# Summing the last four batches of a recurrent block with v on TensorE, in pieces woven among the projections

## The chip, the cores and the metric

The kernel runs on one core of a Trainium2 chip. The metric is device time in microseconds (us) of one execution; several runs are given by their median. The profile comes from one further execution of its own.

## The reference

Eight batches of 256 tokens with 512 channels go through a transformer block (self-attention, cross-attention, MLP) and then an RWKV block, of which the second half of the time is spent. The part that the change touches is its time mixing. For each of 32 heads with 16 channels:

```
def step(s, rkvw):
    r_t, k_t, v_t, w_t = rkvw
    a = k_t[..., :, None] * v_t[..., None, :]
    out = jnp.einsum('bhi,bhij->bhj', r_t, u * a + s)
    s = a + w_t[..., :, None] * s
    return (s, out)
...
_, out = jax.lax.scan(step, s0, rkvw)
out = jnp.moveaxis(out, 0, 1).reshape(b, l, e)
og = out.reshape(b, l, h, s_)
m = og.mean(-1, keepdims=True)
va = ((og - m) ** 2).mean(-1, keepdims=True)
og = ((og - m) / jnp.sqrt(va + 1e-05)).reshape(b, l, e) * gn_w + gn_b
x1 = x + og * g @ Wo.T
...
kk = jnp.square(jax.nn.relu(xk2 @ Wfk.T))
return x1 + rr * (kk @ Wfv.T)
```

r, k, v, w and g are projections of five mixtures of the layer-normalised input; the channel mixing at the end has three more projections (Wfr, Wfk, Wfv).

## The kernel before

Tokens of a batch lie in chunks of 16. Time mixing takes a batch through these stages, all written for the "time" set of buffer slots:

- `a`: layer norm, the shifted difference and the small tanh products that make the mixtures.
- `b` and `e`: the projections g and k, then v, w and r (`proj_t`, `proj_n`, three matmuls a product by `mm3`, L185 to L187). Each result goes to DRAM in a layout by head groups.
- `c`: reads k, r, w back with (head group, chunk) on partitions and makes, inside every chunk, the matrix A of scores between its 16 positions. POOL multiplies into a scratch tile X (L713, L714, L724, L737), DVE reduces X into A (L715, L730, L743), POOL scales r and k by decays (L747 to L749). Then the sum of A with v: 16 POOL products of growing width (L755, 64 up to 1,024 elements a partition) and a DVE reduction behind each (L762). Results go back to DRAM: `ks`, `r0`, `dd` and the in-chunk output `on` (L766, L770).
- `d`: the part between chunks. Small 32x32 TensorE products make each chunk's update of the state (L807), a DVE scan runs over the chunks (L824), small products apply r to the states (L834), DVE adds them to the in-chunk output that was read back (L837), and a group normalisation without the scale follows, written to `yg`.
- `f` and `g`: channel mixing, "chan" slots. `f` reads `yg`, gates it, projects with Wo (L185 to L187 into `o`), adds the residual (L902), layer-normalises (two POOL instructions, L197 and L198) and splits; `g` has the three large projections and the store of the output. In the first `f` the four weights of 512x512 are loaded and split in two parts (L171, L172).

Everything is written in Python in the order of `SEQ`; each entry is a stage letter and a batch. Two numbers decide the real order: the stage's priority, which is batch plus `AT[stage]` times 1,000 (the lower, the more urgent), and the scheduler that puts every instruction into its engine's queue when its inputs are there by the scheduler's own estimate of time. On the chip each queue is then run in that order. `c` and `d` have the most urgent values (-9.5 and -9.3), `f` and `g` late ones (6.25 and 7.75). All DMAs are issued from SP's queue. Buffers are named slots: `in:a16-a19` are the four tiles that a `c` reads, `staged` tiles come from a pool of two.

Of the kernel before, what the change touches and what calls it, by code (L numbers as in the profile page):

```python
# [10 lines left out]
ALU = mybir.AluOpType  # L11
# [6 lines left out]
P = 128  # L18
# [21 lines left out]
def slots(text):  # L40

    r = {}
    for item in text.split():
# [18 lines left out]
        "in:a16-a19 ob:a12 vm:a20,a21 r0t:a22 sts:a23 on_:a2 "  # L62
# [9 lines left out]
    "a0 b0 a1 e0 c0 b1 a2 e1 c1 d0 b2 a3 e2 c2 d1 b3 a4 e3 c3 d2 b4 a5 e4 c4 d3 b5 a6 e5 c5 d4 b6 a7 e6 c6 d5 b7 "  # L72
    "e7 c7 f0 d6 f1 g0 d7 f2 g1 f3 g2 f4 g3 f5 g4 f6 g5 f7 g6 g7"
# [12 lines left out]
PACE = 1000  # L86

# [5 lines left out]
def block_kernel(ctx: ExitStack, tc: tile.TileContext, a: dict, out: bass.AP):  # L93
# [162 lines left out]
    def proj_t(w, xt, emit, kind="o", noc=4, pairs=False):  # L256

        (wh, wl), (xh, xl) = w, xt
        for o2 in range(noc // 2):
            o = bank(kind, [P, 2, T])  # L260
            for oo in range(2):
                oc = 2 * o2 + oo
                cs = slice(oc * P, (oc + 1) * P)
                for k in range(KC):
                    mm3(o[:, oo, :], wh[:, k, cs], wl[:, k, cs], xh[:, k, :], xl[:, k, :], k == 0, k == KC - 1)
                if not pairs:
                    emit(oc, o[:, oo, :])
            if pairs:
                emit(slice(2 * o2, 2 * o2 + 2), o)

    def proj_n(ws, xts, emit, kind="o"):

        for t in range(2):
            ts = slice(t * P, (t + 1) * P)
            o = bank(kind, [P, D])
            n = len(ws)
            for u in range(n):
                (wh, wl), (xh, xl) = ws[u], xts[u]
                for k in range(KC):
                    mm3(o, xh[:, k, ts], xl[:, k, ts], wh[:, k, :], wl[:, k, :], u == 0 and k == 0, u == n - 1 and k == KC - 1)  # L280
            emit(t, o)
# [257 lines left out]
    class TimeMix:  # L539
# [119 lines left out]
        def e(self, b, got):  # L659
# [28 lines left out]
        def c(self, b, got):  # L688
# [3 lines left out]
            def from_dram(src):  # L692
                d_ = wt("in", [P, 16, 64])
# [3 lines left out]
            kb, rb, wb = (from_dram(z) for z in (kd, rd, wd))  # L697

            vt = wt("in", [P, 64, 16])
            for h in range(2):  # L700
                vh = staged([P, 8, 64])
                nc.sync.dma_start(out=vh, in_=vd.rearrange("e (c t) d -> (e c) t d", t=16)[:, 8 * h : 8 * h + 8, :])
                S.copy(vt[:, :, 8 * h : 8 * h + 8].rearrange("p d s -> p s d"), vh)


            A = wt("A", [P, 16, 16, 4])

            def part(t, s_, dims):
                return bass.AP(A.tensor, A.offset + 64 * t + 4 * s_, [A.ap[0], *dims])
# [5 lines left out]
            V.tensor_reduce(part(0, 0, [[68, 16], [1, 4]]), X.rearrange("p (t g i) -> p t g i", t=16, i=16), AX.X, ALU.add)  # L715


            for m in (1, 2, 4, 8):
                nb = 8 // m
                R, K, Wd = (z.rearrange("p (n u) d -> p n u d", n=nb) for z in (rb, kb, wb))  # L720
                if m < 4:
                    for i in range(m):
# [7 lines left out]
                        V.tensor_reduce(part(m + i, 0, [[136 * m, nb], [1, 4 * m]]), X.rearrange("p (n g i) -> p n g i", n=nb, i=16), AX.X, ALU.add)  # L730
                else:
                    ni = 16 // m
                    for n in range(nb):
                        for i in range(0, m, ni):
# [8 lines left out]
                            V.tensor_reduce(part(t0, s0, [[64, ni], [1, 4 * m]]), X.rearrange("p (n g i) -> p n g i", n=ni, i=16), AX.X, ALU.add)  # L743
# [7 lines left out]
            ob = wt("ob", [P, 16, 64])  # L751
            for t in range(16):
                n = t + 1
                Y = wt("X", [P, 1024])[:, : 64 * n] if t else ob[:, 0, :]
                G.tensor_tensor(  # L755
                    Y.rearrange("p (h j s) -> p h j s", h=4, j=16),
                    A[:, t, 0:n, :].rearrange("p s h -> p h s").unsqueeze(2).broadcast_to([P, 4, 16, n]),
                    vt[:, :, 0:n].rearrange("p (h j) s -> p h j s", j=16),
                    ALU.mult,
                )  # L760
                if t:
                    V.tensor_reduce(ob[:, t, :], Y.rearrange("p (d s) -> p d s", s=n), AX.X, ALU.add)  # L762
# [8 lines left out]
            return back(kb, "ks"), back(rb, "r0"), dd, vd, back(ob, "on")  # L771

        def d(self, b, got):

            ksd, r0d, dd, vd, ond = got
# [50 lines left out]
            for q in range(4):  # L826
# [9 lines left out]
                for par in range(2):  # L836
                    V.scalar_tensor_tensor(ov, op.rearrange("p t g c j -> p (t g) c j")[:, :, par], pm[:, 2 + par : 3 + par], ov, ALU.mult, ALU.add)  # L837

# [117 lines left out]
    def mix(n):  # L956
        for _ in range(min(n, len(seq))):
# [3 lines left out]
            with tc.high_priority(tc.cur_priority - base[0] - int(PACE * (b + AT[stage]))):  # L961
                if stage in "fg":
# [12 lines left out]
    mix(len(seq))  # L975

# [51 lines left out]
```

## Time and profile before

| what | us |
|---|---|
| median of 3 runs | 1974.78 |
| lowest and highest | 1973.81, 1986.49 |
| the profiled execution's own time | 1982.31 |
| its span, first to last instruction | 1980.5 |
| stage `c` on POOL, first instruction of batch 0 and last of batch 7 | 1239.2 and 1794.4 |
| the same for batches 4 to 7 | 1520.5, 1588.9, 1662.1, 1727.9 (starts) |
| last large product of `e` for batch 7 | 1638.9 |
| `yg` of batch 7 written | 1833.4 |
| last four periods of channel mixing | about 33 each |

"Busy" is the time in which an engine has an instruction; a matmul's end is modelled, so neighbouring matmuls overlap in the rows and the distance between two starts is what one costs. The granted clock is the share of full speed that TensorE had. A window row has, after its length, each engine's busy time and instructions, then granted clock, DMA share and GB/s.

### The profile page before, as it was taken

The numbers are of one execution on the slowest core, as the hardware profiler recorded it, in microseconds if no ns is written. First come the engines' busy times: TensorE is split into PE (matmuls) and PEld (weight loads), VectorE is DVE, ScalarE is ACT, GpSimd is POOL, SyncE is SP. The second block draws the span as 40 slices with busy tenths as digits, with TensorE's granted clock in tenths as the row PEclk, the third lists the DMA queues.
The fourth block names the chain that finished last, engine by engine and source line by source line (L and its number), as shares of the span: only waits on it lengthen the run. The fifth ranks groups of instructions, "written<-read, shape, count | busy, mean of one in ns | idle before, by whom it ended". The sixth has DMA issues, their size and how long they took to land.

```text
span 1980.5 us, 38765 instructions
## 1 busy us (share of the span) xinstructions
PE 1756.4 (89%) x14576; PEld 1471.8 (74%) x14576; DVE 1379.7 (70%) x3211; ACT 1106.5 (56%) x2745; POOL 747.5 (38%) x550
## 2 busy tenths in 40 slices
PE   4999999989999998999999988888889895789877
PEld 4777777777777776799999976676777673677766
DVE  4777777776778687665654454669678788888554
ACT  3877777887778688532332334354464454355342
POOL 2111111121221221232311100898899999992000
PEclk9999999999999999999999998988898886888888
DMA  6644444656555556322311133454556476442210
GB/s 189 158 125 119 118 118 125 190 142 164 132 146 143 133 135 207 110 90 69 107 65 64 54 128 103 116 142 125 157 138 165 130 195 184 142 108 97 75 64 22
DMA packets 237170, 247.35 MB, mean 125 GB/s; under 512 B 156292, under 2 KB 159244, under 8 KB 236983
## 3 DMA queue, kind: packets, MB, share of 16 engines
q1 hardware_dynamic: 236982, 244.87, 44.7%
q8 instruction: 115, 1.88, 0.4%
q14 instruction: 73, 0.59, 0.1%
HBM read 118.71 MB, written 58.98 MB: 90 GB/s over the span
## 4 chain that ended last, share of the span: by engine, by line
PE 60%; DVE 15%; DMA 6%; ACT 6%; POOL 5%; issue 3%; SPq 3%; POOLq 0%; DVEq 0%; ACTq 0%
PE o L185 8%; PE o L186 8%; PE o L187 8%; PE mm L185 5%; PE mm L186 4%; PE mm L187 4%; PE tr L366 3%; PE out L187 3%; PE out L186 3%; PE out L185 3%; DVE e L359 3%; POOL X L755 2%; PE cx L375 2%; DVE e L357 2%; PE sc L355 2%
## 5 line engine op out<-in xcount | busy, mean ns | idle before, releaser
L362 ACT ACTIVATE e<-e,mx 128x256 f32<-128x256 f32 x512 | 256.7, 506 | 43.0 <-DVE mx L359 42.0
L357 DVE TENSOR_TENSOR e<-sc,mc 128x512 f32<-128x512 f32 x256 | 172.1, 683 | 111.8 <-PE sc L355 56.2
L227 POOL TENSOR_TENSOR u<-y,u 128x1024 fp32r<-128x1024 f32 x32 | 78.5, 2452 | 440.8 <-ACT u L226 440.6
L359 DVE CUSTOM_DVE_ANT_0 e<-e,mn 128x256 f32<-128x256 f32 x512 | 220.6, 473 | 1.0
L755 POOL TENSOR_TENSOR X<-A,in 128x128 f32<-128x128 f32 (+14 forms) x120 | 209.3, 1779 | 14.7 <-DVE ob L762 12.4
L185 PE MATMUL o<-whi,s 128*128 128x512 f32 x320 | 148.4, 464 | 49.4 <-ACT s L890 31.8
L366 PE MATMUL tr<-ident,e 128*128 128x128 f32 x1024 | 174.7, 285 | 18.0 <-ACT e L362 14.7
L185 PE MATMUL mm<-u,whi 128*128 128x256 f32 x512 | 153.7, 301 | 14.3 <-DVE s L319 7.8
L370 ACT COPY pt<-tr 128x512 f32<-128x512 f32 x256 | 147.0, 582 | 34.6 <-PE tr L366 33.9
L366 PEld LDWEIGHTS tr<-ident,e 128*128 128x128 f32 x1024 | 122.3, 144 | 49.2 <-ACT e L362 24.2
L186 PE MATMUL mm<-u,whi 128*128 128x256 f32 x512 | 147.5, 288 | 4.0 <-POOL u L227 4.0
L185 PE MATMUL o<-u,whi 128*128 128x256 f32 x512 | 144.7, 287 | 3.1 <-ACT whi L171 1.6
L187 PE MATMUL mm<-u,wlo 128*128 128x256 f32 x512 | 147.0, 287 | 0.0
L186 PE MATMUL o<-u,whi 128*128 128x256 f32 x512 | 144.0, 283 | 0.0
L187 PE MATMUL o<-u,wlo 128*128 128x256 f32 x512 | 144.0, 283 | 0.0
L186 PE MATMUL o<-wlo,s 128*128 128x512 f32 x320 | 141.4, 442 | 0.0
L293 POOL TENSOR_TENSOR xr<-xr,row 128x512 f32<-128x512 f32 x48 | 65.7, 1388 | 186.0 <-DMA xr<-in_x 81.1
L355 PE MATMUL sc<-stk 128*128 128x256 f32 x512 | 118.0, 322 | 19.3 <-DVE e L357 13.9
L187 PE MATMUL o<-whi,s 128*128 128x512 f32 x320 | 134.4, 438 | 0.6 <-DVE s L891 0.5
L507 ACT ACTIVATE hf<-o,cv 128x256 f32<-128x256 f32 x128 | 59.8, 475 | 117.8 <-PE o L187 115.0
L197 POOL TENSOR_SCALAR rstd<-mv 128x2 f32<-128x2 f32 x48 | 17.2, 357 | 281.2 <-DVE mv L195 260.5
L185 PEld LDWEIGHTS o<-whi,s 128*128 128x128 f32 x320 | 70.0, 219 | 68.8 <-ACT s L890 33.3
(324 smaller groups left out, 5296.3 us busy)
## 6 DMA issues: line engine op xcount, KB each, us to landing
stk<-s SPq DMA_DIRECT2D x512, 128.0 KB, 2.4
x<-x SPq DMA_DIRECT2D x40, 512.0 KB, 4.7
x<-xr SPq DMA_DIRECT2D x24, 512.0 KB, 3.6
xr<-x SPq DMA_DIRECT2D x16, 512.0 KB, 4.8
w<-in_w SPq DMA_DIRECT2D x16, 512.0 KB, 6.7
w<-v SPq DMA_DIRECT2D x32, 256.0 KB, 3.2
x<-in_x SPq DMA_DIRECT2D x8, 512.0 KB
xr<-in_x SPq DMA_DIRECT2D x8, 512.0 KB, 3.6
```

The lines of the kernel that those rows point to most:

```text
L185: TE.matmul(o, ah, bh, start=first, stop=False)
L186: TE.matmul(o, ah, bl, start=False, stop=False)
L187: TE.matmul(o, al, bh, start=False, stop=last)
L227: (eng or V).tensor_tensor(lo, y, r32(hi), ALU.subtract)
L293: G.tensor_tensor(x[:, t, :], x[:, t, :], r, ALU.add)
L355: TE.matmul(sc[:, t, :], qs[hm][:, hc, t * P : (t + 1) * P], ks[hm][:, hc, :], start=True, stop=True)
L357: V.tensor_tensor(e, sc, mc, ALU.mult)
L359: V.tensor_tensor_reduce(e[:, t, :], e[:, t, :], mn[:, t, :], 1.0, 3.0e38, ALU.add, ALU.min, accum_out=mx[:, kk2, hc, t : t + 1])
L362: S.activation(pr[:, t, :], e[:, t, :], AF.Exp, bias=mx[:, kk2, hc, t : t + 1], scale=-1.0, accum_out=sums[:, kk2, hc, t : t + 1])
L366: TE.transpose(pt_ps[:, kk, t * P : (t + 1) * P], pr[:, t, kk * P : (kk + 1) * P], ident)
L370: S.copy(pt, pt_ps)
L755: G.tensor_tensor(Y.rearrange("p (h j s) -> p h j s", h=4, j=16), A[:, t, 0:n, :].rearrange("p s h -> p h s").unsqueeze(2).broadcast_to([P ...
```

## The change

Batches 0 to 3 stay as they were. For batches 4 to 7 (`LATE = 4`):

- `c` no longer loads v, and its 16 products with v (L755) and 16 reductions (L762) are gone. A is laid out the other way round (source position outermost, then head, then target position); one A tile is shared by the four batches, and set to zero once on POOL. It is written to DRAM (`own`) in place of `on`.
- `d` becomes a generator, `steps`. It reads A back with (chunk, source position) on partitions, spreads it with ScalarE into two masked halves (`Ax`, two instructions a half of the tokens), and TensorE multiplies it with v: 32 heads, four 32-row products each, for both halves of the tokens, 256 products of 32x32 by 32x16 a batch (`inside`). ScalarE copies the sum into `o`, where it was read from DRAM before. The rest of `d` (updates, scan, `across`, normalisation) is kept.
- `steps` stops at each `yield` with a number of columns. `between`, called behind each triple of large matmuls, counts the columns that those streamed and lets the next piece be written when the number is reached. A woven piece so takes the priority of the stage in which it is written. `finish(b)` writes out what is left before `f` of that batch.
- `SEQ` has `d4` behind `a7`, `d5` behind `c7`; the slots of the tiles that `c` reads get names of their own on the same addresses.

```diff
-        "in:a16-a19 ob:a12 vm:a20,a21 r0t:a22 sts:a23 on_:a2 "
+        "kb:a16 rb:a17 wb:a18 vt:a19 ob:a12 At:a19 Ax:a12 vm:a20,a21 r0t:a22 sts:a23 on_:a2 "
...
-    "a0 b0 a1 e0 c0 b1 a2 e1 c1 d0 b2 a3 e2 c2 d1 b3 a4 e3 c3 d2 b4 a5 e4 c4 d3 b5 a6 e5 c5 d4 b6 a7 e6 c6 d5 b7 "
-    "e7 c7 f0 d6 f1 g0 d7 f2 g1 f3 g2 f4 g3 f5 g4 f6 g5 f7 g6 g7"
+    "a0 b0 a1 e0 c0 b1 a2 e1 c1 d0 b2 a3 e2 c2 d1 b3 a4 e3 c3 d2 b4 a5 e4 c4 d3 b5 a6 e5 c5 b6 a7 d4 e6 c6 b7 e7 c7 "
+    "d5 f0 f1 g0 d6 f2 g1 d7 f3 g2 f4 g3 f5 g4 f6 g5 f7 g6 g7"
...
+LATE = 4
...
+    woven, columns = [], [0]
+    def between(n):
+        columns[0] += n
+        while woven and columns[0] >= woven[0][1]:
+            columns[0] -= woven[0][1]
+            was, phase[0] = phase[0], "time"
+            woven[0][1] = next(woven[0][2], None)
+            if woven[0][1] is None:
+                woven.pop(0)
+            phase[0] = was
+    def weave(b, steps):
+        if not woven:
+            columns[0] = 0
+        woven.append([b, 0, steps])
+    def finish(b):
+        while woven and woven[0][0] <= b:
+            columns[0] = woven[0][1]
+            between(0)
...
                     mm3(o[:, oo, :], wh[:, k, cs], wl[:, k, cs], xh[:, k, :], xl[:, k, :], k == 0, k == KC - 1)
+                    between(3 * T)
...
                     mm3(o, xh[:, k, ts], xl[:, k, ts], wh[:, k, :], wl[:, k, :], u == 0 and k == 0, u == n - 1 and k == KC - 1)
+                    between(3 * D)
...
                 TE.matmul(tp_[0:64, 0, :], d1[:, k, :], y[:, k, :], start=k == 0, stop=k == KC - 1)
+                between(4 * T)
...
+            late = b >= LATE
+            if not late:
...
+            if b <= LATE:
+                self.A = wt("A", [P, 1024])
+            if b == LATE:
+                G.memset(self.A, 0.0)
+            A = self.A
+            st_, ss, sh = (1, 64, 16) if late else (64, 4, 1)
...
-            ob = wt("ob", [P, 16, 64])
-            for t in range(16):
-                n = t + 1
-                Y = wt("X", [P, 1024])[:, : 64 * n] if t else ob[:, 0, :]
-                G.tensor_tensor(
-                    Y.rearrange("p (h j s) -> p h j s", h=4, j=16),
-                    A[:, t, 0:n, :].rearrange("p s h -> p h s").unsqueeze(2).broadcast_to([P, 4, 16, n]),
-                    vt[:, :, 0:n].rearrange("p (h j) s -> p h j s", j=16),
-                    ALU.mult,
-                )
-                if t:
-                    V.tensor_reduce(ob[:, t, :], Y.rearrange("p (d s) -> p d s", s=n), AX.X, ALU.add)
+            if not late:
+                At = A.rearrange("p (t s h) -> p t s h", t=16, s=16)
+                ob = wt("ob", [P, 16, 64])
...
+            if late:
+                own = dtile(f"ad_{b}", [P, 16, 64])
+                nc.sync.dma_start(out=own, in_=A.rearrange("p (s x) -> p s x", s=16))
+            return back(kb, "ks"), back(rb, "r0"), dd, vd, own if late else back(ob, "on")
...
+            if b >= LATE:
+                return weave(b, self.steps(b, got))
...
+        def steps(self, b, got):
+            ksd, r0d, dd, vd, ad = got
+            dn = staged([16, D])
+            nc.sync.dma_start(out=dn.rearrange("c (e d) -> c e d", e=8), in_=dd.rearrange("e c d -> c e d"))
+            s0t = wt("s0t", [P, KC, 16])
+            nc.sync.dma_start(out=s0t, in_=a["ctx"][b, 2:18, :].rearrange("r (a j) -> (r a) j", j=16).rearrange("(g p) j -> p g j", p=P))
+            ks = [self.n_tile(ksd, t, "ks") for t in range(2)]
+            At = wt("At", [P, 2, 8, 64])
+            for t in range(2):
+                nc.sync.dma_start(out=At[:, t], in_=ad.rearrange("(e u c) s x -> u (c s) e x", e=8, u=2)[t])
+            r0 = [self.n_tile(r0d, t) for t in range(2)]
+            o = wt("on_", [P, 2, D])
+            yield 8 * T
+            dt_ps = bank("wtp", [P, KC, 16])
+            for k in range(KC):
+                TE.transpose(dt_ps[:, k, :], dn[:, k * P : (k + 1) * P], ident[:16, :16])
+            dts = wt("dts", [P, KC, 16])
+            G.memset(dts[:, :, 0:1], 0.0)
+            S.copy(dts[:, :, 1:16], dt_ps[:, :, 0:15])
+            centred(s0t.rearrange("p g j -> p (g j)"), KC, bank("wtp", [P, KC]))
+            sts = wt("sts", [P, KC, 32, 16])
+            for hp in range(2):
+                S.activation(sts[:, :, 16 * hp : 16 * hp + 16, 0], s0t, AF.Copy, scale=pm[:, hp : hp + 1])
+            r0t = wt("r0t", [P, KC, T])
+            yield 4 * T
+            for k2 in range(2):
+                tp = bank("wtp", [P, 2, T])
+                for kk in range(2):
+                    for t in range(2):
+                        TE.transpose(tp[:, kk, t * P : (t + 1) * P], r0[t][:, (2 * k2 + kk) * P : (2 * k2 + kk + 1) * P], ident)
+                S.copy(r0t[:, 2 * k2 : 2 * k2 + 2, :], tp)
+                if not k2:
+                    yield 8 * T
+            vms, vns = [], []
+            for t in range(2):
+                vms.append(wt("vm", [P, 2, D]))
+                vns.append(self.n_tile(vd, t))
+                for par in range(2):
+                    S.activation(vms[t][:, par, :], vns[t], AF.Copy, scale=pm[:, 2 + par : 3 + par])
+            def spread(t):
+                Ax = wt("Ax", [P, 32, 2, 16])
+                for par in range(2):
+                    S.activation(Ax[:, :, par, :], At[:, t].rearrange("p e (h t) -> p (e h) t", t=16), AF.Copy, scale=pm[:, 2 + par : 3 + par])
+                return Ax
+            yield 28 * T
+            for r_ in range(4):
+                rws = slice(32 * r_, 32 * r_ + 32)
+                up = bank("up", [P, 2, KC, 2, 32])
+                for t in range(2):
+                    for g in range(KC):
+                        for q in range(4):
+                            ch = slice(g * P + 32 * q, g * P + 32 * q + 32)
+                            TE.matmul(up[32 * q : 32 * q + 32, t, g], ks[t][rws, ch], vms[t][rws, :, ch], start=True, stop=True)
+                for t in range(2):
+                    c0 = 1 + 8 * t + 2 * r_
+                    n = min(2, 16 - c0)
+                    for hp in range(2):
+                        js = slice(16 * hp, 16 * hp + 16)
+                        S.activation(sts[:, :, js, c0 : c0 + n].rearrange("p g j c -> p g c j"), up[:, t, :, 0:n, js], AF.Copy, scale=pm[:, hp : hp + 1])
+                if r_ == 3:
+                    Ax = spread(0)
+                yield 9 * T
+            for g in range(KC):
+                dT = bank("up", [P, 32, 16])
+                S.copy(dT, dts[:, g, :].unsqueeze(1).broadcast_to([P, 32, 16]))
+                sv = sts[:, g].rearrange("p j c -> p (j c)")
+                V.tensor_tensor_scan(sv, dT.rearrange("p j c -> p (j c)"), sv, 0.0, ALU.mult, ALU.add)
+            def inside(t):
+                av = bank("wtp", [P, D])
+                for h in range(32):
+                    js = slice(16 * h, 16 * h + 16)
+                    for pr in range(4):
+                        rws = slice(32 * pr, 32 * pr + 32)
+                        TE.matmul(av[rws, js], Ax[rws, h].rearrange("p c t -> p (c t)"), vns[t][rws, js], start=True, stop=True)
+                    if h % 4 == 3:
+                        if h == 31:
+                            S.copy(o[:, t, :], av)
+                        yield 5 * T
+            def across(q):
+                rws = slice(32 * q, 32 * q + 32)
+                op = bank("up", [P, 2, KC, 2, 32])
+                for t in range(2):
+                    for g in range(KC):
+                        for pr in range(4):
+                            c0 = 8 * t + 2 * pr
+                            at = t * P + 32 * pr
+                            TE.matmul(op[32 * pr : 32 * pr + 32, t, g], r0t[rws, g, at : at + 32], sts[rws, g, :, c0 : c0 + 2].rearrange("p j c -> p c j"), start=True, stop=True)
+                    if t and q:
+                        chosen(q, op)
+                    elif t:
+                        first.append(op)
+                    yield 6 * T
+            def chosen(q, op):
+                ov = o.rearrange("p t (g q j) -> p (t g) q j", q=4, j=32)[:, :, q]
+                for par in range(2):
+                    V.scalar_tensor_tensor(ov, op.rearrange("p t g c j -> p (t g) c j")[:, :, par], pm[:, 2 + par : 3 + par], ov, ALU.mult, ALU.add)
+            first = []
+            yield from inside(0)
+            Ax = spread(1)
+            yield from across(0)
+            yield from inside(1)
+            chosen(0, first[0])
+            for q in range(1, 4):
+                yield from across(q)
+            self.normed(b, o)
...
+                if stage == "f":
+                    finish(b)
...
+    finish(len(jobs))
```

More of the change, by code (lines that the diff above doesn't have):

```diff
@@ L690, in c, with from_dram @@
             rd, kd, vd, wd = got
-            def from_dram(src):
-                d_ = wt("in", [P, 16, 64])
+            def from_dram(src, name):
+                d_ = wt(name, [P, 16, 64])
                 nc.sync.dma_start(out=d_, in_=src.rearrange("e (c t) d -> (e c) t d", t=16))
                 return d_
[L697 to L706, printed above, removed]
+            kb, rb, wb = (from_dram(z, n) for z, n in ((kd, "kb"), (rd, "rb"), (wd, "wb")))
+            late = b >= LATE
+            if not late:
+                vt = wt("vt", [P, 64, 16])
+                for h in range(2):
+                    vh = staged([P, 8, 64])
+                    nc.sync.dma_start(out=vh, in_=vd.rearrange("e (c t) d -> (e c) t d", t=16)[:, 8 * h : 8 * h + 8, :])
+                    S.copy(vt[:, :, 8 * h : 8 * h + 8].rearrange("p d s -> p s d"), vh)
+            if b <= LATE:
[4 more added lines that the diff above has]
+            st_, ss, sh = (1, 64, 16) if late else (64, 4, 1)
             def part(t, s_, dims):
-                return bass.AP(A.tensor, A.offset + 64 * t + 4 * s_, [A.ap[0], *dims])
+                return bass.AP(A.tensor, A.offset + st_ * t + ss * s_, [A.ap[0], *dims])
             X = wt("X", [P, 1024])
@@ L714, in c @@
             G.tensor_tensor(X3, X3, W["ubc"].unsqueeze(1).broadcast_to([P, 16, 64]), ALU.mult)
-            V.tensor_reduce(part(0, 0, [[68, 16], [1, 4]]), X.rearrange("p (t g i) -> p t g i", t=16, i=16), AX.X, ALU.add)
+            V.tensor_reduce(part(0, 0, [[st_ + ss, 16], [sh, 4]]), X.rearrange("p (t g i) -> p t g i", t=16, i=16), AX.X, ALU.add)
             for m in (1, 2, 4, 8):
@@ L729, in c @@
                         )
-                        V.tensor_reduce(part(m + i, 0, [[136 * m, nb], [1, 4 * m]]), X.rearrange("p (n g i) -> p n g i", n=nb, i=16), AX.X, ALU.add)
+                        V.tensor_reduce(part(m + i, 0, [[2 * m * (st_ + ss), nb], [ss, m], [sh, 4]]), X.rearrange("p (n g i) -> p n g i", n=nb, i=16), AX.X, ALU.add)
                 else:
@@ L742, in c @@
                             )
-                            V.tensor_reduce(part(t0, s0, [[64, ni], [1, 4 * m]]), X.rearrange("p (n g i) -> p n g i", n=ni, i=16), AX.X, ALU.add)
+                            V.tensor_reduce(part(t0, s0, [[st_, ni], [ss, m], [sh, 4]]), X.rearrange("p (n g i) -> p n g i", n=ni, i=16), AX.X, ALU.add)
                 wl_ = Wd[:, :, m - 1 : m, :]
@@ L749, in c @@
                 G.tensor_tensor(wr_, wr_, wl_, ALU.mult)
-            ob = wt("ob", [P, 16, 64])
-            for t in range(16):
-                n = t + 1
-                Y = wt("X", [P, 1024])[:, : 64 * n] if t else ob[:, 0, :]
-                G.tensor_tensor(
-                    Y.rearrange("p (h j s) -> p h j s", h=4, j=16),
-                    A[:, t, 0:n, :].rearrange("p s h -> p h s").unsqueeze(2).broadcast_to([P, 4, 16, n]),
-                    vt[:, :, 0:n].rearrange("p (h j) s -> p h j s", j=16),
-                    ALU.mult,
-                )
-                if t:
-                    V.tensor_reduce(ob[:, t, :], Y.rearrange("p (d s) -> p d s", s=n), AX.X, ALU.add)
+            if not late:
+                At = A.rearrange("p (t s h) -> p t s h", t=16, s=16)
+                ob = wt("ob", [P, 16, 64])
+                for t in range(16):
+                    n = t + 1
+                    Y = wt("X", [P, 1024])[:, : 64 * n] if t else ob[:, 0, :]
+                    G.tensor_tensor(
+                        Y.rearrange("p (h j s) -> p h j s", h=4, j=16),
+                        At[:, t, 0:n, :].rearrange("p s h -> p h s").unsqueeze(2).broadcast_to([P, 4, 16, n]),
+                        vt[:, :, 0:n].rearrange("p (h j) s -> p h j s", j=16),
+                        ALU.mult,
+                    )
+                    if t:
+                        V.tensor_reduce(ob[:, t, :], Y.rearrange("p (d s) -> p d s", s=n), AX.X, ALU.add)
             def back(src, name):
@@ L770, in c @@
             nc.sync.dma_start(out=dd.rearrange("e c d -> (e c) d"), in_=wb[:, 15, :])
-            return back(kb, "ks"), back(rb, "r0"), dd, vd, back(ob, "on")
+            if late:
+                own = dtile(f"ad_{b}", [P, 16, 64])
+                nc.sync.dma_start(out=own, in_=A.rearrange("p (s x) -> p s x", s=16))
+            return back(kb, "ks"), back(rb, "r0"), dd, vd, own if late else back(ob, "on")
         def d(self, b, got):
+            if b >= LATE:
+                return weave(b, self.steps(b, got))
             ksd, r0d, dd, vd, ond = got
@@ L837, in d @@
                     V.scalar_tensor_tensor(ov, op.rearrange("p t g c j -> p (t g) c j")[:, :, par], pm[:, 2 + par : 3 + par], ov, ALU.mult, ALU.add)
+            self.normed(b, o)
[103 more added lines that the diff above has]
+                yield from across(q)
+            self.normed(b, o)
@@ L839, in d, with normed @@
+        def normed(self, b, o):
             oh = heads(o)
```

## The prediction

> **What bounds the kernel now.** I read the page first: the engines' shares, the slices of 49.5 us and the chain of waits.
>
> ```profile
> span 1980.5 us, 38765 instructions
> PE 1756.4 (89%) x14576; PEld 1471.8 (74%) x14576; DVE 1379.7 (70%) x3211; ACT 1106.5 (56%) x2745; POOL 747.5 (38%) x550
> PE   4999999989999998999999988888889895789877
> ...
> POOL 2111111121221221232311100898899999992000
> PEclk9999999999999999999999998988898886888888
> ...
> PE 60%; DVE 15%; DMA 6%; ACT 6%; POOL 5%; issue 3%; SPq 3%; POOLq 0%; DVEq 0%; ACTq 0%
> ```
>
> POOL is full from slice 25 to 36, where the eight `c` run back to back, and idle afterwards. Yet the chain that ends last holds 60% PE and 5% POOL: the `c` of batch 7 ends at 1794.4, its `yg` is stored at 1833.4, and the stage that reads it comes near 1900. So POOL is full, but has some 60 us to spare at the end. PE has its worst slices at 34 and 35 (5 and 7 tenths, clock 8 and 6). I cut the second half into windows at the places where PE's work changes:
>
> ```profile
> 1520.40:1643.00 122.60, 107.69 (x1415) 86.53 (x1416) 100.56 (x159) 61.47 (x130) 113.50 (x79) 0.84 0.65 180
> 1643.00:1681.00 38.00, 15.55 (x288) 11.81 (x288) 30.39 (x49) 18.59 (x39) 36.63 (x22) 0.59 0.62 164
> 1681.00:1822.00 141.00, 118.43 (x1717) 97.57 (x1715) 119.75 (x214) 70.13 (x154) 108.78 (x74) 0.88 0.41 122
> 1822.00:1855.00 33.00, 27.10 (x136) 22.43 (x136) 23.45 (x53) 14.87 (x29) 0.93 (x2) 0.86 0.25 80
> 1855.00:1888.00 33.00, 27.64 (x136) 22.88 (x136) 18.36 (x34) 13.34 (x27) 0.93 (x2) 0.86 0.18 61
> ```
>
> Columns: length, busy time of PE, weight loads, DVE, ACT, POOL, then clock, DMA share, GB/s. PE idles 14.9 us in the first, 22.4 us in the second (while channel mixing starts), 22.6 us in the third, about 6 us in each period of the tail. The bound is PE with the waits in its in-order queue. What waits in the second window, from the timelines of PE and of POOL:
>
> ```profile
> 1649.92 0.79 PE L185 MATMUL o<-whi,s 128*128 128x512 f32 x1 [6.47 <-DVE x L902]
> ...
> 1665.46 0.61 PE L780 MATMUL wtp<-ident,w 16*128 16x16 f32 x4 [11.13 <-DMA w<-dd]
> ```
>
> ```profile
> 1659.81 1.20 POOL L197 TENSOR_SCALAR rstd<-mv 128x2 f32<-128x2 f32 x1
> 1662.08 3.25 POOL L713 TENSOR_TENSOR X<-in 128x1024 f32<-128x1024 f32 x1 [1.07 <-DVE ob L762]
> 1665.29 0.70 POOL L198 TENSOR_TENSOR rstd<-rstd,nhalf 128x2 f32<-128x2 f32 x1
> ```
>
> The layer norm of the first `f` has its statistics at 1656.8 and its last POOL instruction at 1666.0: two short instructions (0.92 us in the quiet tail) stand behind products of `c`. The 11.13 us are `d5` waiting for `c5`.
>
> **The change, removed.** Batches 4 to 7 lose 107.3 us of POOL (L755 in their four windows) and 45.3 us of DVE (L762). A late `c` does not shrink by all 26.8 us: those products covered the reload. In `c4`, r goes back at 1559.1, 38.6 us after its first instruction; the next k is requested at 1564.95 and a load of that kind lands 3.7 us later, so the next `c` starts some 48.5 us after the last instead of 68.5. Four starts move: `c5` at 1569, `c6` 1618, `c7` 1666 (the r of `e7`, written from 1645.6 in 4.1 us, is there), `c7` done near 1705, 90 us sooner. Each loses two v loads (SP 0.3 to 0.5 us each) and two ACT copies of 1.10 us; each `d` keeps 11 DMAs, the two reads of A (nearest row: 256 KB, 3.9 us) in place of two of `on`.
>
> **Added on PE.** A plain float32 product is two instructions here: L807 is written 128 times a batch and the profile counts 2,048 for eight. So `inside` is 512 instructions a batch, in 16 pieces of 32. Rows of small products:
>
> ```profile
> 1471.30 0.99 PE L807 MATMUL up<-vm,ks 32*32 32x64 f32 x64
> 1472.22 0.33 PE L217 MATMUL wtp<-ident,w 128*128 128x128 f32 x1
> ...
> 1475.22 1.89 PE L807 MATMUL up<-vm,ks 32*32 32x64 f32 x128
> 1477.04 0.66 PE L217 MATMUL wtp<-ident,w 128*128 128x128 f32 x4
> ```
>
> From start to next start 64 cost 0.92 us and 128 cost 1.82, so one costs 14.1 ns. The new ones stream 16 columns instead of 64 against weights of equal size: between a quarter, 3.5 ns, and 14.1; I take 9, the middle. A change between large and small products: the burst starts 0.09 us later than the next large one would, and a burst of 16 of L834 took 0.59 us where 16 at its 24.9 ns make 0.40; so 0.11 to 0.28 us a piece, taken as 0.2. A piece is 32 x 9 ns + 0.2 = 0.49 us; 16 of them 7.8; six further breaks in the old bursts 1.2: 9.0 us a batch, 36 us in all. Bounds: 17 us (3.5 ns and 0.11 a piece) and 76 us (L834's 24.9 ns, 0.28).
>
> [...]
>
> **Added elsewhere, at nothing.** ACT: four spreads (row L795, 0.72 us) and two copies of `av` (L816, 0.61) against 2.2 us saved, +1.9 us a batch, on an engine 50% busy; uncovered 8 us. POOL: one zeroing of A, twice a 0.53 us row. SP: the writing of A is read back through DRAM; a piece that is early stalls the loads of `f` queued behind it. The new wait: v stays in both `staged` buffers until the second `inside` is done, so the next batch's `dd` and r loads stand in SP's queue with `yg`, `g` and x of channel mixing behind them. I price it at 0, as the woven order asks for the next batch only then; uncovered it is the 11.13 us of the row above, once per batch from 5 on: 33 us.
>
> **Given back.** (1) 1643 to 1681: `c5` is done at 1608 instead of 1662, so the 13.5 us of PE of `d5` (an eighth of L807 and L834, 11.3, and eight transposes of 0.27) and its 9 new ones can lie in the 22.4 idle us; I take 17, from 0 (ordered elsewhere) to 22. (2) The layer norms of `f0` (9.2 us) and `f1` (1711.9 to 1717.4) no longer stand behind L755: 13 us of latency over the quiet 0.9, of which 6 on PE's path, from 0 to 13. (3) 1681 to 1822: `d6` and `d7` are free to fill 22.6 idle us, and waits for scans (8.2 us there and before) get other work between: 11, 0 to 22. (4) 1520 to 1643: DVE falls by 11 of 100 us: 5, 0 to 12. (5) The tail's 6 us a period take the last pieces of `d7`: 4, 0 to 11. (6) Clock 0.59 and 0.88: the twelve L185 to L187 products from 1649.92 took 4.4 us against 3.1 for the twelve at 1640.39; fewer gaps give 10, 0 to 20. Sum 53.
>
> Net 36 - 53 = -17. The profiled execution took 1982.3 us (span 1980.5 and 1.8 around it), so 1965.3; the median of the runs lies 7.5 below the profiled one: **1958 us**.
>
> **Rivals.** (A) The forecast, 1930 to 1980, chance 0.50. (B) Slower: PE is the bound and the pieces pay. Place: PE's queue from 1681 to 1855; price 36 us, none covered because the order written beforehand does not meet the gaps of the chip (the 11.13 us wait shows that orders and chip differ): 1975 + 36 = 2011, up to 2051 at the upper price. It decides once the give-backs fall under 16 us. For it: clock and PE at 118 of 141; against: 60 us of idle time in three windows. 0.26. (C) POOL's chain was the bound after all, through the queues that wait on it (SP waited 48.5 us for r's scaling): four starts 20 us sooner with pieces at their cheapest, 1975 - 80 + 17 = 1912. Against: 5% of the chain. 0.12. (D) It does nothing: the gaps are waits inside channel mixing (33 us a period with or without `c`), pieces fit exactly: 1975, from 1960 to 1990. 0.12.
>
> **How the numbers follow.** One per cent, about what tells from no change, is 20 us: 1955 and 1995. Below 1955 lie C and a little over half of A (0.28): 0.40. Above 1995 lies B, with 0.01 of D: 0.27. Between: 0.33. The range leaves out the lower part of C (0.08) and the upper half of B (0.12): 1915 to 2012.
>
> **What would show it.** Right: `c` starts 48 to 50 us apart for batches 5 to 7; PE busy over 30 of the 38 us around the first `f`; the two rstd instructions within 2 us; a `d` of 22 to 23 us of PE. Wrong: `inside` at 14 ns or more an instruction, gaps before L185 as long as before, SP waiting for `staged` buffers, or clock under 0.85 after 1681.

## The result, and the profile after

The changed kernel takes 2010.6 us (four runs, 2006.6 to 2015.3), the kernel before, beside it, 1976.7: a ratio of 1.0166, 95% interval 1.0137 to 1.0195, or +33 us. The forecast was 1958. The profiled execution took 2008.3 us, its span is 2006.5.

The page of the changed kernel: span, engines, slices of PE and of the clock, the chain's shares.

```profile
span 2006.5 us, 42742 instructions
PE 1777.2 (89%) x16624; PEld 1487.4 (74%) x16624; DVE 1347.3 (67%) x3151; ACT 1114.7 (56%) x2761; POOL 639.6 (32%) x487
PE   4899999999999997999999988897898867889877
...
PEclk9999999999999998999999998898988966789989
...
PE 65%; DVE 14%; ACT 8%; POOL 4%; DMA 4%; issue 4%; SPq 2%; DVEq 0%; POOLq 0%; ACTq 0%
```

POOL lost 107.9 us; DVE lost 44.6 of reductions, of which some 12 came back in lines that the change doesn't touch. PE has 2,048 products more, its share of the chain went from 60% to 65%, and the clock row has 6, 6, 7 in slices 33 to 35, where projections and channel mixing meet. The first four windows of before, in the kernel after (length; PE, weight loads, DVE, ACT, POOL; clock, DMA share, GB/s):

```profile
1520.40:1643.00 122.60, 95.52 (x1629) 81.22 (x1624) 80.96 (x125) 46.56 (x102) 94.77 (x67) 0.79 0.52 142
1643.00:1681.00 38.00, 22.74 (x748) 16.73 (x748) 26.15 (x38) 22.99 (x45) 12.72 (x9) 0.55 0.94 280
1681.00:1822.00 141.00, 122.52 (x2219) 98.43 (x2210) 89.05 (x166) 71.83 (x152) 37.88 (x30) 0.82 0.32 91
1822.00:1855.00 33.00, 33.00 (x638) 24.65 (x638) 19.18 (x38) 13.68 (x27) 0.93 (x2) 1.00 0.10 35
```

In the first three windows PE is busy for 240.8 us, against 241.7 before; weighted by length, the clock is 0.77 against 0.83. With more instructions to run, TensorE got no more busy time and a lower clock. From 1822 on, 184 us are left where 158 were left before: most of the loss shows before that point.

What PE waits for is told by its waits from 1500 us on (us in total, times, longest). "issue" is a wait for nothing that the profile shows. Before the change PE has no such wait there at all. After it:

```profile
PE wtp L967 <- issue: 12.4, 7, 4.0
...
PE wtp L917 <- issue: 5.1, 2, 3.8
```

With those of the updates, of `across` and of an early `d` they make 24.8 us. L967 is the new `inside`, L917 the transposes of r in `steps`. PE's timeline in one of these places (start, length, and in brackets the idle time before):

```profile
1624.57 1.91 PE L967 MATMUL wtp<-w,Ax 32*32 32x16 f32 x128 [2.42 <-issue]
1628.32 0.34 PE L967 MATMUL wtp<-w,Ax 32*32 32x16 f32 x10 [1.84 <-issue]
...
1630.83 0.80 PE L211 MATMUL o<-whi,s 128*128 128x512 f32 x1
1631.42 0.63 PE L212 MATMUL o<-wlo,s 128*128 128x512 f32 x1
```

Two things are to be seen. The pieces are not among large products here: 448 calls of `d4`, two products each, stand in one run from 1598.9 to 1630.3. A likely reason, not shown, is that its pieces were written behind large products that had been queued long before, and became ready together. And where nothing else holds the run up, it stops after every 128 products. Behind it the large products start 0.43 us apart at a granted clock of 0.50, where 0.23 us is their distance at 1.00 (1692.08, 1692.32, 1692.55 in the same timeline). `d5` follows in long runs from 1647 to 1688, ahead of the last projection of batch 7, whose last large product ends near 1699 instead of 1638.9. The longest wait inside `d5` is one for data: 7.2 us for its scan.

### The profile page after: what moved, and what is told of

Same layout as the page of the kernel before. It is cut to its first block, busy times and chain, and to the rows that moved or that the text cites. A ratio compares the mean times of both kernels' runs of the same rounds, so it can differ in the third digit from the quotient of the medians.

```text
span 2006.5 us, 42742 instructions
## 1 busy us (share of the span) xinstructions
PE 1777.2 (89%) x16624; PEld 1487.4 (74%) x16624; DVE 1347.3 (67%) x3151; ACT 1114.7 (56%) x2761; POOL 639.6 (32%) x487
## 4 chain that ended last, share of the span: by engine, by line
PE 65%; DVE 14%; ACT 8%; POOL 4%; DMA 4%; issue 4%; SPq 2%; DVEq 0%; POOLq 0%; ACTq 0%
PE o L211 9%; PE o L212 8%; PE o L213 8%; PE mm L211 5%; PE mm L212 4%; PE mm L213 4%; PE tr L394 3%; PE out L213 3%; PE out L211 3%; PE out L212 3%; DVE e L387 3%; PE cx L403 2%; PE sc L383 2%; DVE e L385 2%; PE tp L243 2%
## 5 line engine op out<-in xcount | busy, mean ns | idle before, releaser
L211 PE MATMUL o<-whi,s 128*128 128x512 f32 x320 | 144.4, 451 | 39.4 <-ACT s L1057 27.6
L213 PE MATMUL o<-whi,s 128*128 128x512 f32 x320 | 133.8, 435 | 0.3 <-DVE s L1058 0.3
L774 POOL TENSOR_TENSOR X<-rb,kb 128x1024 f32<-128x1024 f32 x48 | 113.4, 2385 | 7.2 <-DVE A L780 7.0
L383 PEld LDWEIGHTS sc<-stk 128*128 128x128 f32 x512 | 81.8, 197 | 42.6 <-DVE e L385 24.8
```

What stands on the lines that cost most here:

```text
L211: TE.matmul(o, ah, bh, start=first, stop=False)
L213: TE.matmul(o, al, bh, start=False, stop=last)
L383: TE.matmul(sc[:, t, :], qs[hm][:, hc, t * P : (t + 1) * P], ks[hm][:, hc, :], start=True, stop=True)
L774: G.tensor_tensor(X.rearrange("p (i s d) -> p i s d", i=ni, s=m), rb[:, t0 : t0 + ni, :].unsqueeze(2).broadcast_to([P, ni, m, 64]), kb[:, ...
```

## The experiments

Ratios are to the kernel before, run beside each; 0.001 is 2 us. Theories in the expectations: S, dense small products are held up by the supply of instructions; O, the order delays the projections of batch 7; W, the price is plain TensorE work.

### Order, products and operand size

`late8` keeps the new order and slots and no late batch (`LATE = 8`). `noinside` leaves the in-chunk sum out for batches 4 to 7; `bf16` gives its operands as bf16, so that a call is one instruction (`bench` has 512 products for 512 calls, 1,024 in float32) and the sum is less exact; `late6` has two late batches.

```diff
-LATE = 4
+LATE = 8        # late8; 6 in late6
...
+                TE.matmul(av, ident, vns[t], start=True, stop=True)      # noinside, in place of:
-                        TE.matmul(av[rws, js], Ax[rws, h].rearrange("p c t -> p (c t)"), vns[t][rws, js], start=True, stop=True)
...
-                Ax = wt("Ax", [P, 32, 2, 16])
+                Ax = wt("Ax", [P, 32, 2, 16], BF16)                      # bf16, v likewise
```

> The changed kernel with no late batch: the new order of stages and the new slot names alone, all eight batches summed with v on POOL. If the loss comes from the small products and how they run (theories S, O, W below), this stands near the kernel before: 1970 to 1985 us. If the new order of stages costs it, it stays near 2010. S: PE runs out of instructions in dense runs of small products, because a block of 256 instructions takes about 3.7 us to come (128 small products with their weight loads take 1.9 us to run). O: the pieces were not woven on PE; those of batches 4 and 5 stand in runs of hundreds before the last projection of batch 7, which ends 60 us later than before. W: plain work, 9 ns a product and 0.2 us a piece, as predicted, with no cover.

Measured 1978.9, ratio 1.0001 (0.9973 to 1.0030): order and slots by themselves cost nothing that these runs can tell (6 us either way).

> The changed kernel without the small products with v: one large product of the identity with v stands in for the 128 calls of each half of a batch, so that part of the output is left out; loads, spreading, pieces and order of stages stay. S: 16 blocks of 256 instructions less, of which about half fell in runs with nothing beside them, so 25 to 35 us less than the changed kernel (1975 to 1985), and the runs of the other small products still show waits for instructions. W: 36 us less, 1975. O: the updates and the products across chunks of batches 4 and 5 still stand before the last projection, so only 10 to 20 us less (1990 to 2000).

Measured 1968.9, ratio 0.9957 (0.9932 to 0.9982), below all three expectations. Without the small products the change would win 8 us; so the products cost 41 us in this order (1.0166 less 0.9957). Between the two profiles, from 1500 us on, PE is idle for 25 us less without them (67.9 against 93.3) and busy for 14 less. The unexplained waits fall from 25 to 5 us, and from 1520.4 to 1822 the clock is 0.85 instead of 0.77.

> The changed kernel with both operands of the products with v in bf16: one instruction instead of two a call, one copy of v more on ACT (0.6 us) a half; the sum is less exact. Same pieces, same order of the source. S: 8 blocks of 256 instructions less, about half of what leaving the products out gives: 12 to 18 us less (1992 to 1998). W: the streamed part (9 ns of each) more than halves, the 0.2 us a piece stays: 20 us less. O: under 8 us less.

Measured 1989.5, ratio 1.0057 (1.0036 to 1.0077): half the instructions, half the cost. The 21 us won are what W said; S had 12 to 18. The unexplained waits of PE fall from 24.8 to 13.1 us.

> Only batches 6 and 7 are late; 4 and 5 go as before. In the trace of the changed kernel the pieces of 6 and 7 stand among large products without a gap, those of 4 and 5 in dense runs. S and O: the loss came from 4 and 5, so it is gone, 1965 to 1985. W: half of the work stays, half of the loss: 1990 to 1995.

Measured 2011.9, ratio 1.0169 (1.0127 to 1.0211), as slow as with four late batches, outside all three expectations. The windows of `late6` show where:

```profile
1810.00:1820.00 10.00, 4.64 (x250) 4.46 (x248) 9.64 (x16) 7.54 (x18) 0.00 (x0) 0.50 0.01 3
...
1830.00:1840.00 10.00, 10.00 (x115) 6.09 (x107) 1.72 (x3) 1.07 (x2) 0.00 (x0) 0.50 0.01 2
```

The clock falls to 0.50 in a dense run of `d6`, 272 calls from 1801.6 on, and the pieces that follow, well woven, run at half clock until past 1850 although PE is busy all the time from 1820 on. The second and third outputs lie 65 us apart there, 31 before the change. But the supply of instructions is not what empties PE here: from 1500 us on the unexplained waits of `late6` are 1.8 us in all, against 24.8 in the changed kernel. In this run PE waits mostly for data:

```profile
1813.33 1.35 PE L967 MATMUL wtp<-w,Ax 32*32 32x16 f32 x83 [0.44 <-issue]
1819.60 1.47 PE L982 MATMUL up<-sts,r0t 32*32 32x64 f32 x32 [4.92 <-DVE sts L958]
```

So a loss of this size can come about almost without the stops, and S alone does not explain the loss. In the changed kernel itself the same weave runs at clock 1.00 (the window from 1822). Why the clock did not come back here isn't settled.

### The small products by themselves

`bench` appends stretches to the kernel before, when nothing else runs. It was executed once.

```diff
+    stage("fa", "k6", run16)      # 512 calls, 32x32 by 32x16, float32
+    stage("fb", "k7", run16b)     # the same in bf16
+    stage("fc", "k6", run64)      # 512 calls by 32x64, float32
+    stage("fd", "k7", woven)      # 33 triples of large products, 16 calls between each two
+    stage("fe", "k6", alone)      # 33 triples, then 128 calls
```

> The kernel before, and behind its last large product five measured stretches on TensorE with nothing else running: 512 calls of 32x32 by 32x16 in float32 (1,024 instructions), the same in bf16 (512), 512 calls of 32x32 by 32x64 in float32 (1,024), 33 triples of large products with 16 calls of the first kind between each two (1,024 instructions in 32 pieces), and 33 triples alone with 128 calls behind them. Its output is that of the kernel before. Theory S (a dense run of small products is held up by the supply of instructions, a block of 256 in about 4 us): 1,024 take 32 us with 16 and with 64 columns alike, 512 in bf16 16 us, stops of 2 us or more every 128 products; between large products the same 1,024 add only 11 to 14 us. Theory W (the price is plain TensorE work): 1,024 take 11 to 15 us everywhere, 512 in bf16 half of it, no stops. Theory O (order: the stops were waits for data): as W. If the supply is slow only while other transfers fill the DMA engines: blocks every 2 us, 1,024 in 16 us.

PE's timeline in the first stretch, which begins 0.33 us behind the kernel's last large product:

```profile
1979.05 2.43 PE L991 MATMUL fa<-ident 32*32 32x16 f32 x268
1983.43 1.26 PE L991 MATMUL fa<-ident 32*32 32x16 f32 x128 [1.95 <-issue]
1987.17 1.91 PE L991 MATMUL fa<-ident 32*32 32x16 f32 x128 [2.48 <-issue]
1990.66 1.91 PE L991 MATMUL fa<-ident 32*32 32x16 f32 x128 [1.58 <-issue]
```

268 products run without a stop, then there is one after every 128. From start to start of these blocks it takes 3.5 to 4.0 us (the next begins at 1994.69), and so it does in bf16 (2005.39, 2009.14, 2013.17) and with 64 columns (2027.90, 2031.92): the work differs, the number of instructions does not. The stops are 1.6 to 2.8 us long with 16 columns and 0.4 to 2.0 with 64, where the work fills more of a block. 128 products are, with a weight load each, 256 instructions. The pages count them too, as transfers of the instruction queue (number, MB, share); first before, then after the change:

```profile
q8 instruction: 115, 1.88, 0.4%
```

```profile
q8 instruction: 131, 2.15, 0.4%
```

Sixteen transfers more for 2,048 products and as many weight loads: about 256 instructions each. From 1985 on hardly anything else moves (a DMA share of 0.01, below), so it is not contention. That the stop is a wait for instructions is inferred from these counts; the profile doesn't name it. For dense runs S holds, though the whole was shorter than it said (1,024 in 24.7 us instead of 32, as the first 268 did not wait).

How the clock went is in the windows of `bench`, the last one with 64 columns:

```profile
1970.00:1979.00 9.00, 8.59 (x44) 6.45 (x43) 4.17 (x6) 1.92 (x4) 0.00 (x0) 1.00 0.01 2
...
1985.00:1995.00 10.00, 4.12 (x279) 3.91 (x283) 0.00 (x0) 0.00 (x0) 0.00 (x0) 0.50 0.01 3
...
2040.00:2049.00 9.00, 5.49 (x328) 4.97 (x317) 0.00 (x0) 0.41 (x1) 0.00 (x0) 1.00 0.02 5
```

Full clock before, half once the stops have come with 16 columns, where PE is busy for 41% of the time; full clock again with 64 columns, where it is busy for 61% between stops of 1.5 to 1.8 us. So stops as such did not halve it here. And the woven stretch:

```profile
2069.80 0.44 PE L991 MATMUL fd<-ident 32*32 32x16 f32 x32
2070.18 0.97 PE L1022 MATMUL big<-wide,ident 128*128 128x512 f32 x3
```

No stops here (there is one of 1.1 us at 2050.64, and half clock from about 2053 to 2059 with PE busy), and the next pieces begin at 2071.07, 2072.34 and 2073.61. A period is 1.27 us; three large products alone take 0.69 (102 of them from 2092.98 on, 0.23 apart). So a piece of 16 calls costs 0.58 us at full clock: 0.37 to 0.38 its own, 0.2 the change to and from large products. The prediction had 0.49. The 32 pieces so add 19 us, where S had 11 to 14 and W 11 to 15.

### Weaving less, later, and truly

`flat` writes each late `d` in one go. `woven` queues a piece behind the large product that it was written behind. `tail` moves the late `d` back in the written order.

```diff
-                return weave(b, self.steps(b, got))
+                return [None for _ in self.steps(b, got)] and None       # flat
...
-            woven[0][1] = next(woven[0][2], None)
+            with tc.issue_after(last.ins) if last is not None else nullcontext():
+                woven[0][1] = next(woven[0][2], None)                    # woven
...
+    "... a6 e5 c5 b6 a7 e6 c6 b7 e7 c7 f0 d4 f1 g0 d5 f2 g1 d6 f3 g2 d7 f4 ..."   # tail
```

> The changed kernel with each late d written out in one go at its place in the order, so that nothing is woven and the runs of small calls in the queue are 64 to 448 long for all four batches. S: four d of 512 calls at about 29 ns an instruction in place of 14, some 15 us of stops each: 2015 to 2030. W: the changes between large and small products go (64 pieces of 0.2 us): 1995 to 2000. O: d5 stands before e of batch 7 as in the changed kernel: 2005 to 2015.

Measured 2027.0, ratio 1.0255 (1.0220 to 1.0290): as S said. The unexplained waits rise to 35 us.

> The changed kernel with one order added: a piece is queued only behind the large product that it is written behind. The longest runs of small calls are 223, 278 and 256 instead of 448, 224 and 235, and e of batch 7 is not held up by d5. S: a few runs shorter, 2000 to 2010. W: 2005 to 2015. O: batch 7's last large product of e about 40 us sooner, 1975 to 1990.

Measured 2015.4, ratio 1.0199 (1.0156 to 1.0242): no gain, and nothing for O, as `c` of batch 7 started 30 us sooner (1675.2 instead of 1705.2) without a benefit. Its order still had runs of 223 to 278 calls, and on the chip `d4` was again one run of 448 (896 products from 1599.5 on), which the expectation did not have. The unexplained waits rose to 36 us.

> The changed kernel with the four late d moved back in the order, behind f0, f1, f2 and f3, where their pieces find large products of channel mixing; runs of small calls are mostly 1 to 64 long, the longest 109, 138, 164 and 112. O: e of batch 7 ends near 1640 as before the change and the four d cost what the idle time of TensorE leaves: 1970 to 1985. S: only four long runs, stops of some 10 us in all: 1980 to 1990. W: the instructions cost the same wherever they stand: 2005 to 2015.

Measured 1997.1, ratio 1.0098 (1.0062 to 1.0134), 13 us better than the change, between the expectations. But its unexplained waits are 25 us as before. The trace shows one reason: `d4` did not move on the chip. It is one run of 448 calls again, from 1594.5 on, with 12 of the 25 us in it, and the expectation's longest runs, 109 to 164, are those of the other three batches. So `tail` moves at most these, and it does not test S as meant.

`after2` and `tail2` also queue the next large product behind the piece, so that no run is longer than 32 calls; `tail2bf` does that with bf16 operands.

```diff
-        TE.matmul(o, ah, bh, start=first, stop=False)
+        with tc.issue_after(piece[0].ins) if piece[0] is not None else nullcontext():
+            TE.matmul(o, ah, bh, start=first, stop=False)
```

> The changed kernel with the same order of stages, but truly woven: a piece is queued behind the large product it was written behind, and the next large product behind the piece. Runs of small calls in TensorE's queue are 16 to 32 long everywhere (448, 224 and 235 before). S: the stops before small products of the late batches, some 28 us, go: 1980 to 1990. W: the products' own 30 us stay, and the stops were hidden anyway: 2005 to 2012. O: as S, if e of batch 7 ends before 1650, else 2010.

> The kernel with the late d moved behind f0 to f3, truly woven in the same way (pieces of 16 and 32 calls). S: its remaining stops (19 us of idle time before the in-chunk products) go: 1975 to 1985. W: 1995 to 2000. O: as without the weaving, 1995 to 2000.

> The same with both operands of the products with v in bf16, so that a call is one instruction; the in-chunk sum is less exact by that. S and W alike: half of the 30 us of the products' own work goes, 15 us below the float32 version; under S that is 1962 to 1970, under W 1980 to 1985.

Measured 2076.9, 2075.2 and 2058.9, ratios 1.0478 (1.0444 to 1.0513), 1.0448 (1.0397 to 1.0499) and 1.0386 (1.0351 to 1.0421). All expectations fail. The stops before `inside` are gone (one wait for nothing of 10.6 us, before a transpose, is left in `after2`), and the time is 66 us worse than with them. One reason is in PE's timeline of `after2`, at full clock:

```profile
1749.93 0.40 PE L217 MATMUL o<-whi,s 128*128 128x512 f32 x1
1750.26 0.44 PE L971 MATMUL wtp<-w,Ax 32*32 32x16 f32 x32
1750.63 0.50 PE L214 MATMUL o<-whi,s 128*128 128x512 f32 x1
1750.97 0.40 PE L216 MATMUL o<-wlo,s 128*128 128x512 f32 x1
```

From start to next start a large product takes 0.23 us among its like, 0.33 ahead of a piece and 0.34 behind one. In `after2` 131 large products of 512 columns and 81 of 256 stand beside a piece after 1500 us (54 and 18 in the changed kernel). Without idle time they take 0.43 and 0.23 us on the mean, where 0.23 and 0.12 is the usual distance: 35 us more in sum, against 9 in the changed kernel, slower stretches at half clock included. PE's idle time grew by 8 us. The rest of the 66 us was not taken apart. Half the instructions brought 12 us in `tail2bf` (1.0448 less 1.0386), uncertain by as much.

### POOL's relief, and weaving, each alone

`free` is the kernel before without the products with v, their reductions and the loads of v in batches 4 to 7; the in-chunk output is zero there. `weaveonly` and `tailweave` weave `d` in the order of the change and of `tail`, with POOL's products as before. `tailnoin` and `tailbf` are `noinside` and `bf16` in the order of `tail`.

```diff
+            if b >= 4:
+                G.memset(ob, 0.0)
-            for t in range(16):
+            for t in range(16 if b < 4 else 0):     # free
...
-            late = b >= LATE
+            late = False                            # weaveonly; steps reads `on` and has no inside
```

> The kernel before with the products with v, their reductions and the loads of v left out for batches 4 to 7 and the in-chunk output set to zero there: POOL and DVE are relieved as in the changed kernel, and nothing is added on TensorE. Give-backs as the prediction summed them, without those that need the new pieces as filling (5 for DVE, 6 for the layer norms, half of 17 for the first f, 5 of 10 for the clock): 1950 to 1955. If POOL's relief brings the chain that ends last nothing: 1968 to 1977.

Measured 1979.5, ratio 0.9997 (0.9978 to 1.0015): the relief of POOL and DVE, alone, is worth nothing, within some 4 us. The shares of the chain that ended last hardly moved (PE 63% and POOL 5%, before 60% and 5%). These are the three windows of `free` that answer to those before:

```profile
1520.40:1643.00 122.60, 99.81 (x1308) 81.22 (x1298) 85.67 (x144) 47.89 (x110) 90.70 (x68) 0.82 0.58 159
1643.00:1681.00 38.00, 32.49 (x451) 24.43 (x451) 34.17 (x38) 21.25 (x40) 25.40 (x15) 0.68 0.95 266
1681.00:1822.00 141.00, 117.39 (x1466) 97.07 (x1465) 99.17 (x203) 70.71 (x154) 38.12 (x30) 0.83 0.32 95
```

The gap around the first `f` did fill: 32.5 us of PE instead of 15.6. The window before it emptied by 8, and the clock fell on both sides (0.82 and 0.83 from 0.84 and 0.88): 8 us more of busy time in the three, at a mean clock of 0.81 instead of 0.83. The first output came at 1731.7 (1722.4 before), the last at 1973.0 (1976.6).

> The changed kernel's order and its woven d, but POOL and DVE make the products with v for all eight batches as before, and d reads their result back. If the 8 us of the kernel without the small products came from weaving d: 1966 to 1970, and this beats both kernels. If they came from POOL's relief: 1975 to 1980.

> The same with the late d behind f0 to f3, as in the moved order. From weaving: 1966 to 1970. From POOL's relief: 1975 to 1982, and c of the last batch must still be done before its d is written, which it is (near 1794, d of batch 7 runs behind f3).

Measured 1989.2 and 1988.5, ratios 1.0031 (1.0011 to 1.0051) and 1.0034 (1.0017 to 1.0050): weaving alone costs 6 to 7 us, and neither expectation holds.

> The kernel with the late d moved behind f0 to f3 (1997), with the products with v left out and one 128-row product with the identity for each half in their place: the in-chunk sum is missing for batches 4 to 7. W (2,048 instructions at the 14.5 ns that they cost with their changes in the trace): 30 us less, 1965 to 1970. S with stops left in that order: 1955 to 1960. If the order itself is what costs: 1980 or more.

> The same kernel with the products with v, their operands in bf16, one instruction a call; the in-chunk sum is less exact. W: half of the 30 us, 1980 to 1985. S with stops left: 1975.

Measured 1977.4 and 1983.8, ratios 0.9980 (0.9965 to 0.9996) and 1.0008 (0.9989 to 1.0028). In this order the products cost 23 us (1.0098 less 0.9980), less than the 30 of W, and in bf16 6. No kernel with the whole computation beats the one before.

So the change adds up, one step at a time, in its own order: weaving +6 (`weaveonly`), POOL and DVE relieved -15 (from there to `noinside`, which also spreads A on ScalarE), the small products +41; together +33. In the moved order: +7, -11, +23. Each difference of two ratios is uncertain by 5 to 8 us.

## Why the prediction was wrong, step by step

**Given back, 53 us: the step that failed.** It measured 0 alone (`free`) and 11 to 15 where pieces were there to fill the gaps; weaving `d` cost 6 to 7 more, which the prediction had at nothing. Term by term: (1) the 22.4 idle us around the first `f` were taken for a hole that `d5` fills without cost. In `free` 17 of them were filled as forecast, and the end did not move: the window before emptied and the clock fell beside it. In the changed kernel itself the window holds 22.7 us of PE, not the 30 that were to show the step right. (2) The layer norms' POOL instructions are free of `c` only in the second `f`; POOL's timeline after the change:

```profile
1708.74 0.25 POOL L223 TENSOR_SCALAR rstd<-mv 128x2 f32<-128x2 f32 x1
1713.67 0.73 POOL L224 TENSOR_TENSOR rstd<-rstd,nhalf 128x2 f32<-128x2 f32 x1
```

These are the first `f`'s, 5 us apart, among the instructions of `c7`, which had begun at 1705.2; in the second they stand at 1754.26 and 1754.56. (3) and (4) are in the 11 to 15 us and were not separated. (5) The window from 1822 is full (33.00 of 33) with `d7` at clock 1.00: PE is busy for 6 us more there; forecast were 4. (6) The clock was to rise and fell, to 0.77 over the first three windows and to 0.82 in that from 1681, under the 0.85 named as a sign. Dense runs go with a lower clock, and the prediction had them nowhere. From 1520.4 to 1822 it is 0.77 in the changed kernel, 0.85 without the products (`noinside`) and 0.69 with each `d` in one go (`flat`), where PE is busy for the same 237 us as in `late8` at 0.81. Dense runs are not all: `weaveonly` has 0.78 without the products.

**Added on PE, 36 us: the price was about right, its cover was not.** `inside` took 29.9 us from start to start, 14.6 ns an instruction with its changes (15.3 predicted), a late `d` 22.0 us (22 to 23 predicted). By the prediction's own sign, 14 ns, it counts as dear; but the 41 us of cost hold more than the 30 of work: 19 us of unexplained waits came with the products (24.8 against 5.4 in `noinside`), and a lower clock. How these add up to 41 was not taken apart, as part of them lies beside idle time that was there anyway. The bursts of 64 and 128 that gave 14.1 ns are at most 256 instructions long and did not show the stop: before the change there is none after 1500 us. The upper bound, 76, held all of it.

**Late `c` 48 to 50 us apart: right in place for `c5` and `c6`**, which start at 1570.0 and 1617.9 (forecast 1569 and 1618; 53.7 and 47.9 us apart), wrong for `c7`, 87 us behind `c6`: it waits for the projections of batch 7, which stood behind the dense `d4` and `d5`. Without the products (`noinside`) it follows after 53.9 us. But the delay itself was not the price: `woven` took 30 us of it away and was no faster. That r would be there at 1666 took those as fixed, though the change moves the work in front of them.

**At nothing, SP's wait for `staged`:** it came. SP's waits from 1500 us on, the line of `inside` as releaser of the staged tiles:

```profile
SPq L714 <- PE wtp L967: 11.9, 3, 7.8
```

With the two kinds of transposes in `steps` as releasers it is 30.8 us of SP's time, close to the 33 that stood as the uncovered price. Before the change the same load waited 12.3 us for the transposes and for ScalarE's copies. What of the difference reached PE was not tested.

**The rivals.** B, 2011, has the measured time and its deciding point: the give-backs fell under 16 us. That the number fits so well is luck: B added 36 us with nothing given back, the runs show +6, -15 and +41. It is by B's share of the range, 1915 to 2012, that the measured time lies inside it; the forecast itself had the wrong sign. B's mechanism, pieces that meet no gaps, is part of the answer; dense runs that stop, wait for their own data and go with a lower clock (0.77 against 0.85 in `noinside`) were not among the cases. C, the chain of POOL, is excluded by `free`: POOL was relieved and the end did not move. D failed with the products' cost.

## What to carry to other kernels

Idle time on the bounding engine is not a price list: before booking the relief of another engine, take its work out and see whether the end moves (here 107 us of POOL and 45 of DVE were worth 0 alone, and some 11 to 15 with something to fill the gaps). Where a change adds thousands of tiny instructions to one queue, count them in blocks of the instruction stream (256 instructions here, with a stop of 0.4 to 2.8 us between blocks in `bench`) and look at the order in the trace: a piece written among large products may stand in a run of 448 on the chip, even where the written order was changed to prevent it (`tail`, `woven`). Cutting finer was no cure here: each change between small and large products took 0.2 us, and the kernels with strict order lost 66.

## What the runs showed of the hardware

- Alone (`bench`), TensorE ran at most 268 small products on, then stopped after every 256 instructions, with hardly anything else moving: 1.6 to 2.8 us with 16 columns, 0.4 to 2.0 with 64, and 3.5 to 4.0 us a block, in float32 with 16 and with 64 columns and in bf16 with 16.
- The granted clock fell to 0.50 in runs whose single stops were at most 2.8 us long and PE 41% busy, and was 1.00 between stops of 1.5 to 1.8 us with PE 61% busy (`bench`). It stayed at 0.50 through 30 us in which PE was busy all the time with pieces and large products by turns (`late6`).
